# Two graph-attention layers on one core: six weight buffers, bank-by-bank scores over the transposed weights, two c buffers

## The chip, the cores and the metric

The kernel runs on one core of one Trainium2 chip. The metric is the device time of one execution in microseconds (us). The kernel before the change took 4322.22 us, the median of three runs (4315.53 to 4325.43).

The engines are named as the profile names them: PE (TensorE matmuls, with PEld for its weight loads), DVE (VectorE), ACT (ScalarE), POOL (GpSimd) and SP (SyncE, which issues most DMAs). Each has its own queue and works it in order; they wait for each other through semaphores.

## The reference

`x` is 8 images of 2048 rows and 256 columns, `adj` a 2048 x 2048 mask. Each layer attends over rows, adds its input and normalizes. Cut to what is computed:

```
# layer 0, eight heads of 32 columns
x_proj = einsum('bnd,hdf->bhnf', x, W)
e = leaky_relu(e_src[..., :, None] + e_dst[..., None, :], 0.2)
e = e + softplus(beta_tilde) * log(adj + 1e-6)
e = where(adj > 0, e, most_negative)
h = einsum('bhij,bhjf->bhif', softmax(e), x_proj)
x = layernorm(x + concat_heads(h) @ W_out.T)

# layer 1, one head of 256 columns
e = leaky_relu(einsum('bnd,bmd->bnm', x @ W1, x @ W2), 0.2)
e = where(adj > 0, e, -1e12)
x = layernorm(x + relu(softmax(e) @ (x @ W3)))
```

All of it is float32. Layer 1 of an image needs all rows of that image's layer 0.

## The kernel before, in words

**Layer 0 as units.** The exponential of a leaky ReLU of a sum is written as a maximum of two products, so that no exponential of a 2048 x 2048 matrix is needed. The work is cut into units `(hp, jt)`: a pair of heads `hp` (4 per image) and a tile `jt` of 128 neighbours (16). There are 64 units per image and 512 in all. `Gat.step` makes one: for each of the two heads, DVE computes the 128 x 2048 weights `s` (L375) from a row tile `c` (the heads' query factors, spread over the partitions by a DMA, L313), a scalar per partition `re`, and a transposed mask tile `mt` (1 MB, L202, loaded anew for every unit). PE then multiplies `s` into `val` and `den` (L407, `products`): these are matmuls with 32 columns of weights, four of which run side by side in the array. In `SUMMED` tiles the denominator is instead summed on DVE into `d` (L386), the first one on ACT (L392), and only the sum goes through PE. A unit's two `s` tiles come from a ring with tag "s" of four buffers (L374), so DVE can be two units ahead of PE. A pair of heads reads two `c` tiles in all its 16 units; the ring "c" has three buffers (L312). In the last unit of a pair, right behind each head's L375, the next `c` load is put on SP's queue. `finish` and `output` close a pair and an image (division, projection `y` L477, normalization).

**Layer 1 as row tiles.** `Dot` works on the image whose layer 0 is done, one tile of 128 rows at a time, 16 per image. `scores(it)` makes four banks `e` of 512 columns on PE (L538), ACT writes each through a Prelu into the 128 x 2048 tile `p` (L540), DVE masks it and takes the row maximum in one operation (L543), and ACT takes the exponential (L546). `step` then turns `p` back, 128 x 128 at a time (transposes on PE, L561, copied by ACT into `pts`, L563), multiplies the turned weights into `acc` (L577), and ACT and DVE divide, add and normalize (L582 to L585). Scores are made one row tile ahead: `step` for tile `it` holds `scores(it + 1)`, which writes the other of two `p` buffers. The turned weights have two `pts` buffers, so a turn of bank g + 1 stands on PE between the `acc` matmuls of banks g - 1 and g:

```
pt = turned(0)
...
    self.scores(it + 1)
fill(1)
for g in range(NB):
    now, pt = pt, turned(g + 1) if g + 1 < NB else None
    # 4 acc matmuls from now
fill(2)
```

Every fourth step also makes `h1` for the next four row tiles (`queries`, L528).

**How the two layers interleave.** Image 0 runs its layer 0 alone, together with the projections of all other images (L268) and the making of the masks. From then on, layer 1 of image b - 1 and layer 0 of image b share the queues: `fill(k)` in `Dot.step` calls `layer_0`, which runs so many units of the next image at that place. In the 13 middle row tiles of an image, `n` is 3 or 4 and the units stand as `(0, n - 2, 2)`. Between two images the projections `y`, the turns `tr` and `h3` of the finished layer 0 stand between groups of two units. The last image's layer 1 has nothing beside it (the tail).

**What sets the order.** PE's queue is in program order (a manual schedule), and SP's from image 1 on. The order of DVE and ACT is set by the framework's scheduler, within what the data and buffers allow. Three PSUM banks (`ps`, tag "mm") rotate over all matmul results but `acc`, `val` and `den`.

**Other rings.** Tag "p" (two buffers) holds `p`, and at the start the first rows of x and the mask tiles `m`. Tag "pt" (two) holds `pts` and some start-up tiles. Tag "v" (three) holds the projected values of a head pair, loaded in the middle of the pair before.

Of the kernel before, what the change touches and what calls it, by code (L numbers as in the profile page):

```python
# [27 lines left out]
def kernel(  # L28
# [50 lines left out]

    def mm_tile(name):  # L80
        return ps.tile([P, BK], F32, tag="mm", name=name)
# [43 lines left out]
    first_x = [wide.tile([P, NT // 2, D], F32, tag="p", name="xr", bufs=2) for _ in range(2)]  # L125
# [8 lines left out]
    def later_weights():  # L134

        nc.sync.dma_start(w3s, w3.rearrange("(k p) d -> p k d", p=P))
        w1t, w2t = (chunk.tile([P, KC, D], F32, tag="pt", name=name, bufs=2) for name in ("w1t", "w2t"))
# [40 lines left out]
    def make_m(jt):  # L178
# [3 lines left out]
        m = wide.tile([P, NT, P], F32, tag="p", name="m", bufs=2)  # L182
# [51 lines left out]
    class Gat:  # L234
# [12 lines left out]
        def scores_first(self, xt):  # L247
# [7 lines left out]
            s = chunk.tile([P, BK], F32, tag="pt", name="scores", bufs=2)  # L255
# [46 lines left out]
        def load(self, hp):  # L302
            self.v[hp] = chunk.tile([P, NT, HP * DH], F32, tag="v", name="v", bufs=3)
            nc.sync.dma_start(self.v[hp], v_d[self.b, hp])
# [5 lines left out]
        def query_rows(self, h):  # L310

            c = wide_tile("c", "c", 3)  # L312
            nc.sync.dma_start(c, c_d[self.b, h:h + 1, :].to_broadcast([P, N]))  # L313
            return c

        def load_ahead(self):
# [6 lines left out]
            for _ in range(3):  # L323
                self.cs_ahead.append(next(self.c_loads))
                self.mts.append(next(self.mt_loads))
            self.mts.append(next(self.mt_loads))
# [13 lines left out]
        def step(self, count=1):  # L340

            for _ in range(count):
# [29 lines left out]
                for a in range(HP):  # L372
                    h = hp * HP + a
                    sa = wide_tile("s", "s", 4)  # L374
# [140 lines left out]
    class Dot:  # L515


        def __init__(self, gat):
            self.b, self.x1t, self.h3 = gat.b, gat.x1t, gat.h3
            self.at = 0  # L520
            self.queries(0)
# [10 lines left out]
        def scores(self, it):  # L532
            pen = mask(it, self.b == 0)
            p = wide_tile("p", "p", 2)
            for c in range(NB):
                t = mm_tile("e")
# [10 lines left out]
            self.ahead = p, den  # L547

        def step(self, fill=lambda k: None):


            it, (p, den) = self.at, self.ahead
# [4 lines left out]

            def turned(g):
# [3 lines left out]
                pt = chunk.tile([P, BK], F32, tag="pt", name="pts", bufs=2)  # L562
                nc.scalar.copy(pt, t)  # L563
                return pt

            pt = turned(0)
            if it + 1 < NT:
                if (it + 1) % IG == 0:
                    self.queries((it + 1) // IG)
                self.scores(it + 1)  # L570
            fill(1)
            acc = pacc.tile([P, D], F32, tag="acc", name="acc")
            for g in range(NB):
                now, pt = pt, turned(g + 1) if g + 1 < NB else None
                for k in range(IG):
                    j = g * IG + k
                    nc.tensor.matmul(acc, now[:, ts(k, P)], self.h3[:, j, :], start=(j == 0), stop=(j == NT - 1))  # L577
            fill(2)
# [30 lines left out]
    def others():  # L609
# [18 lines left out]
        for n, (gat, g) in enumerate(groups):  # L628
            if g == 0:
                gat.begin()  # L630
            v = chunk.tile([P, NP, IG, HP * DH], F32, tag="v", name="v", bufs=3)
# [32 lines left out]
    for b in range(1, B + 1):  # L664
# [13 lines left out]
        else:  # L678

            dot.step(lambda k: layer_0((0, 2, 2)[k]))  # L680
# [57 lines left out]
```

The softmax here doesn't subtract the row's maximum and nothing guards it: scores larger than these inputs give would overflow.

## Time and profile before

| What | us |
|---|---|
| median of three runs (lowest, highest) | 4322.22 (4315.53, 4325.43) |
| the profiled execution | 4319.21 |
| its span | 4317.4 |
| PE busy | 4191.7 (97%) |
| DVE busy | 3704.8 (86%) |
| ACT busy | 1657.5 (38%) |
| s operations on DVE (L375), 1024 of them | 2355.5 |
| d operations on DVE (L386), 318 | 738.5 |
| mask operations on DVE (L543), 128 | 292.4 |
| 1 MB loads of mt / of c | 496 / 64 |

The table is of one profiled execution. Its time and its span differ by 1.8 us, which lie around the first and the last instruction. Busy time is what an engine spent inside instructions, and matmul ends are modelled, so a busy PE may still have gaps between the starts of its matmuls. Granted clock of TensorE: 0.994 of full speed over the span. The span has three parts: up to about 560 us image 0, from there to about 3880 us seven times the same cycle of about 475 us, then the tail.

### The profile page before, as it was taken

Reading aid. Unit: us, or ns where it says so; the run is one execution under the profiler, and the core shown is the slowest. Engines: PE = TensorE matmul, PEld = TensorE weight load, DVE = VectorE, ACT = ScalarE, POOL = GpSimd, SP = SyncE. Lnnn points to the kernel's source line nnn. Section 1 sums busy time; section 2 is a strip of 40 time slices with the busy share of each in tenths; the row PEclk is TensorE's granted clock in tenths of the full one; section 3 lists DMA queues with packets and bytes.
Section 4 is the critical chain, followed back from the end, with each engine's and each line's share of the span. In section 5 each row is a group of like instructions: output and inputs, shape, how many; then the busy total and the mean of one; then the engine's idle time right before and its main releaser. Section 6 shows DMA issues by size and latency. Waiting matters only on the chain. (4 is left out here: it accounts for less than half of the span.)

```text
span 4317.4 us, 58896 instructions
## 1 busy us (share of the span) xinstructions
PE 4191.7 (97%) x24640; PEld 2202.1 (51%) x24640; DVE 3704.8 (86%) x2468; ACT 1657.5 (38%) x3019; POOL 9.5 (0%) x14
## 2 busy tenths in 40 slices
PE   7999999999999999999999999999999999999999
PEld 5444455454454545544554544555455445545766
DVE  7878888998899989999899998999899998999222
ACT  7522233333333333333343334333333333433554
POOL 0000000000000000000000000000000000000000
PEclk9999999999999999999999999999999999999999
DMA  8979756666555554556555564555545565544211
GB/s 272 308 258 319 273 198 210 225 229 209 184 191 192 201 203 180 179 184 227 187 193 186 189 207 183 192 190 206 202 176 181 186 226 185 198 171 146 81 50 41
DMA packets 267946, 843.50 MB, mean 195 GB/s; under 512 B 32672, under 2 KB 165792, under 8 KB 193952
## 3 DMA queue, kind: packets, MB, share of 16 engines
q1 hardware_dynamic: 232352, 806.17, 53.0%
q10 hardware_dynamic: 35328, 33.56, 2.3%
q8 instruction: 193, 3.16, 0.3%
q14 instruction: 73, 0.60, 0.0%
HBM read 763.76 MB, written 75.37 MB: 194 GB/s over the span
## 5 line engine op out<-in xcount | busy, mean ns | idle before, releaser
L375 DVE SCALAR_TENSOR_TENSOR s<-c,re,mt 128x2048 f32<-128x2048 f32 x1024 | 2355.5, 2343 | 150.3 <-PE den L407 65.6
L407 PE MATMUL val<-s,v 128*32 128x512 f32 x8192 | 1024.5, 602 | 56.7 <-DVE s L375 56.5
L577 PE MATMUL acc<-h,pts 128*128 128x256 f32 x4096 | 955.9, 381 | 18.5 <-ACT pts L563 18.5
L538 PE MATMUL e<-x1t,h 128*128 128x512 f32 x2048 | 904.0, 594 | 4.6 <-ACT pts L563 4.5
L577 PEld LDWEIGHTS acc<-h,pts 128*128 128x128 f32 x4096 | 746.9, 190 | 119.4 <-ACT pts L563 34.2
L386 DVE SCALAR_TENSOR_TENSOR d<-s,re,d 128x2048 f32<-128x2048 f32 x318 | 738.5, 2342 | 0.0
L407 PE MATMUL den<-s,re 128*32 128x512 f32 x5216 | 664.1, 597 | 0.0
L538 PEld LDWEIGHTS e<-x1t,h 128*128 128x128 f32 x2048 | 379.0, 190 | 451.6 <-issue 413.5
L407 PEld LDWEIGHTS val<-s,v 128*32 128x32 f32 x8192 | 245.5, 110 | 675.0 <-issue 519.9
L563 ACT COPY pts<-pt 128x512 f32<-128x512 f32 x512 | 295.4, 582 | 663.5 <-PE pt L561 660.3
L540 ACT ACTIVATE p<-e 128x512 f32<-128x512 f32 x512 | 302.6, 595 | 426.1 <-PE e L538 412.7
L543 DVE CUSTOM_DVE_ANT_0 p<-p,pen 128x2048 f32<-128x2048 f32 x128 | 292.4, 2284 | 198.7 <-ACT p L540 198.6
L407 PEld LDWEIGHTS den<-s,re 128*32 128x32 f32 x5216 | 181.5, 111 | 396.4 <-issue 394.6
L561 PEld LDWEIGHTS pt<-ident,p 128*128 128x128 f32 x2048 | 238.5, 141 | 214.4 <-issue 173.9
L546 ACT ACTIVATE p<-p,neg 128x2048 f32<-128x2048 f32 x128 | 256.7, 2005 | 232.2 <-DVE neg L543 232.2
L561 PE MATMUL pt<-ident,p 128*128 128x128 f32 x2048 | 317.7, 278 | 0.0
L582 ACT ACTIVATE z<-acc,rec 128x256 f32<-128x256 f32 x128 | 60.7, 474 | 391.6 <-PE acc L577 259.4
L583 DVE TENSOR_TENSOR z<-z,x1r 128x256 f32<-128x256 f32 x128 | 53.8, 420 | 142.9 <-ACT z L582 142.8
L392 ACT ACTIVATE d<-s,re 128x2048 f32<-128x2048 f32 x54 | 107.9, 2011 | 80.0 <-PE den L407 66.3
L268 PE MATMUL proj<-wp,xt 128*128 128x272 f32 (+1 forms) x512 | 132.5, 404 | 4.8 <-ACT v L270 3.2
L528 PE MATMUL h1p<-x1t,w 128*128 128x512 f32 x256 | 117.0, 595 | 9.4 <-ACT x1t L503 9.4
L270 ACT COPY v<-proj 128x256 f32<-128x256 f32 x128 | 47.0, 375 | 202.5 <-PE proj L268 197.5
(88 smaller groups left out, 1919.8 us busy)
## 6 DMA issues: line engine op xcount, KB each, us to landing
mt<-mt_d SPq DMA_DIRECT2D x496, 1024.0 KB
c<-c_d SPq DMA_DIRECT2D x64, 1024.0 KB
pen<-pen_d SPq DMA_DIRECT2D x112, 512.0 KB
xg<-in_x_dram SPq DMA_DIRECT2D x60, 512.0 KB
adj_t<-in_adj_dram SPq DMA_DIRECT2D x16, 1024.0 KB
mt_d<-mt SPq DMA_DIRECT2D x16, 1024.0 KB
rb<-rec_d SPq DMA_DIRECT2D x128, 128.0 KB
x_d<-ht ACTq DMA_DIRECT2D x32, 512.0 KB
```

The costliest lines, as they stand in the source:

```text
L268: nc.tensor.matmul(t[:, 0:cols], xt[:, kc, ts(it % IG, P)], wp[:, kc, 0:cols], start=(kc == 0), stop=(kc == KC - 1))
L375: nc.vector.scalar_tensor_tensor(sa, self.cs[a], self.re[:, 0, jt, h:h + 1], mt, ALU.max, ALU.mult)
L386: nc.vector.scalar_tensor_tensor(d, sa, e[:, jt - 1, h:h + 1], d, ALU.mult, ALU.add)
L407: nc.tensor.matmul(dst[ts(q, DH), ts(c, BK)], weights[q % 2], s[q % 2][:, ds(q // 2 * HALF + c * BK, BK)], start=start, stop=stop)
L528: nc.tensor.matmul(t, w12[:, kc, ts(dc, P)], self.x1t[:, kc, ts(g, BK)], start=(kc == 0), stop=(kc == KC - 1))
L538: nc.tensor.matmul(t, self.h1[:, kc, ts(it % IG, P)], self.x1t[:, kc, ts(c, BK)], start=(kc == 0), stop=(kc == KC - 1))
L540: nc.scalar.activation(p[:, ts(c, BK)], t, AF.Prelu, alpha=ALPHA)
L543: nc.vector.tensor_tensor_reduce(p, p, pen, -1.0, FMAX, ALU.add, ALU.min, neg)
L546: nc.scalar.activation(p, p, AF.Exp, bias=neg, scale=-1.0, accum_out=den)
L561: nc.tensor.transpose(t[:, ts(k, P)], p[:, ts(g * IG + k, P)], ident)
L563: nc.scalar.copy(pt, t)
L577: nc.tensor.matmul(acc, now[:, ts(k, P)], self.h3[:, j, :], start=(j == 0), stop=(j == NT - 1))
```

## The change

The ring of `s` gets six buffers (three units). `p` becomes one tile, kept in the pool `whole`. The four banks of turned weights get a `pts` buffer each. `scores` takes a function that it calls ahead of each bank: in `step` this is `turned`, so that PE turns bank c of the old `p` and then makes bank c of the new scores, whose Prelu writes over the old bank. All 16 `acc` matmuls follow in one piece. `fill` has two places instead of three, and the units of a row tile stand together behind `acc`. To make room, `c` goes from three buffers to two, `v` from three to two, and the first rows of x and the tiles `m` move to the ring "s". `load_ahead` loads two `c` and four `mt` tiles ahead, where it loaded three and four.

The diff, without the repeated renames:

```diff
@@ pools
+    p_all = whole.tile([P, N], F32, tag="p", name="p")
...
-    first_x = [wide.tile([P, NT // 2, D], F32, tag="p", name="xr", bufs=2) for _ in range(2)]
+    first_x = [wide.tile([P, NT // 2, D], F32, tag="s", name="xr", bufs=6) for _ in range(2)]
...
-        m = wide.tile([P, NT, P], F32, tag="p", name="m", bufs=2)
+        m = wide.tile([P, NT, P], F32, tag="s", name="m", bufs=6)
@@ Gat
-            self.v[hp] = chunk.tile([P, NT, HP * DH], F32, tag="v", name="v", bufs=3)
+            self.v[hp] = chunk.tile([P, NT, HP * DH], F32, tag="v", name="v", bufs=2)
...
-            c = wide_tile("c", "c", 3)
+            c = wide_tile("c", "c", 2)
...
-            for _ in range(3):
+            for _ in range(HP):
                 self.cs_ahead.append(next(self.c_loads))
                 self.mts.append(next(self.mt_loads))
-            self.mts.append(next(self.mt_loads))
+            for _ in range(2):
+                self.mts.append(next(self.mt_loads))
...
-                    sa = wide_tile("s", "s", 4)
+                    sa = wide_tile("s", "s", 6)
@@ Dot
+            self.p = p_all
             self.queries(0)
...
-        def scores(self, it):
-            pen = mask(it, self.b == 0)
-            p = wide_tile("p", "p", 2)
+        def scores(self, it, between=lambda c: None):
+            pen, p = mask(it, self.b == 0), self.p
             for c in range(NB):
+                between(c)
                 t = mm_tile("e")
...
-            self.ahead = p, den
+            self.ahead = den
@@ Dot.step
             fill(0)
+            pts = []
             def turned(g):
                 t = mm_tile("pt")
                 for k in range(IG):
                     nc.tensor.transpose(t[:, ts(k, P)], p[:, ts(g * IG + k, P)], ident)
-                pt = chunk.tile([P, BK], F32, tag="pt", name="pts", bufs=2)
+                pt = chunk.tile([P, BK], F32, tag="pt", name="pts", bufs=NB)
                 nc.scalar.copy(pt, t)
-                return pt
-            pt = turned(0)
+                pts.append(pt)
             if it + 1 < NT:
                 if (it + 1) % IG == 0:
                     self.queries((it + 1) // IG)
-                self.scores(it + 1)
-            fill(1)
+                self.scores(it + 1, turned)
+            else:
+                for g in range(NB):
+                    turned(g)
             acc = pacc.tile([P, D], F32, tag="acc", name="acc")
             for g in range(NB):
-                now, pt = pt, turned(g + 1) if g + 1 < NB else None
                 for k in range(IG):
                     j = g * IG + k
-                    nc.tensor.matmul(acc, now[:, ts(k, P)], self.h3[:, j, :], start=(j == 0), stop=(j == NT - 1))
-            fill(2)
+                    nc.tensor.matmul(acc, pts[g][:, ts(k, P)], self.h3[:, j, :], start=(j == 0), stop=(j == NT - 1))
+            fill(1)
@@ the interleaving
-            dot.step(lambda k: layer_0((0, 2, 2)[k]))
+            dot.step(lambda k: layer_0((0, 4)[k]))
...
-        dot.step(lambda k: layer_0((2, 0, 2)[k]))
+        dot.step(lambda k: layer_0((2, 2)[k]))
...
-            dot.step(lambda k: layer_0((0, n - 2, 2)[k]))
+            dot.step(lambda k: layer_0((0, n)[k]))
```

More of the change, by code (lines that the diff above doesn't have):

```diff
@@ L136, in later_weights @@
         nc.sync.dma_start(w3s, w3.rearrange("(k p) d -> p k d", p=P))
-        w1t, w2t = (chunk.tile([P, KC, D], F32, tag="pt", name=name, bufs=2) for name in ("w1t", "w2t"))
+        w1t, w2t = (chunk.tile([P, KC, D], F32, tag="pt", name=name, bufs=NB) for name in ("w1t", "w2t"))
         for w, dst in ((w_out, wot), (w1, w1t), (w2, w2t)):
@@ L254, in scores_first @@
                                      start=(kc == 0), stop=(kc == KC - 1))
-            s = chunk.tile([P, BK], F32, tag="pt", name="scores", bufs=2)
+            s = chunk.tile([P, BK], F32, tag="pt", name="scores", bufs=NB)
             nc.scalar.copy(s, t)
@@ L546, in scores @@
             nc.scalar.activation(p, p, AF.Exp, bias=neg, scale=-1.0, accum_out=den)
-            self.ahead = p, den
+            self.ahead = den
         def step(self, fill=lambda k: None):
-            it, (p, den) = self.at, self.ahead
+            it, p, den = self.at, self.p, self.ahead
             self.at += 1
@@ L630, in others @@
                 gat.begin()
-            v = chunk.tile([P, NP, IG, HP * DH], F32, tag="v", name="v", bufs=3)
+            v = chunk.tile([P, NP, IG, HP * DH], F32, tag="v", name="v", bufs=2)
             for k in range(IG):
```

## The prediction

> **What bounds the kernel now.** I read the busy shares first, then the windows of one image cycle, then the waits inside the stretch in which both layers run, last the groups. Busy time of PE and DVE over the whole span:
>
> ```profile
> PE 4191.7 (97%) x24640; PEld 2202.1 (51%) x24640; DVE 3704.8 (86%) x2468; ACT 1657.5 (38%) x3019; POOL 9.5 (0%) x14
> ```
>
> PE looks like the only limit, but DVE's 86% is an average over a first image and a tail in which it has little to do. From 560 to 3880 us seven images pass, each in about 475 us (3320 / 7). One of them, cut at its mask operations (L543): first the thirteen row tiles that carry 44 layer-0 units, then the change of images (columns: us, then busy us of PE, PEld, DVE, ACT, POOL):
>
> ```profile
> 2145.30:2488.70 343.40, 339.80 (x1951) 173.57 (x1953) 332.58 (x213) 129.41 (x227) 0.00 (x0) 1.00 0.52 187
> 2488.70:2620.00 131.30, 122.72 (x789) 63.47 (x782) 111.27 (x77) 45.13 (x77) 0.00 (x0) 0.99 0.60 209
> ```
>
> In the long part DVE works 332.6 of 343.4 us and PE 339.8: **two engines at their limits**, coupled by four s buffers, that is two units of lead. In the short part both have holes. Who waits for whom from 560 to 3880 us:
>
> ```profile
> DVE z L583 <- ACT z L582: 73.7, 37, 3.4
> DVE p L543 <- ACT p L540: 67.7, 16, 9.4
> DVE s L375 <- DMA mt<-mt_d: 43.0, 22, 4.9
> ...
> DVE s L375 <- DMA c<-c_d: 4.3, 5, 3.1
> ...
> PE val L407 <- DVE s L375: 40.5, 33, 3.3
> PE acc L577 <- ACT pts L563: 17.9, 34, 1.3
> PE h1p L528 <- ACT x1t L503: 9.4, 7, 1.5
> PE e L538 <- ACT pts L563: 4.5, 6, 1.0
> ```
>
> PE's waits come to about 74 us, the first for s, the second for the copy of transposed weights. The c loads are almost free today (4.3 us). The groups that set the prices:
>
> ```profile
> L375 DVE SCALAR_TENSOR_TENSOR s<-c,re,mt 128x2048 f32<-128x2048 f32 x1024 | 2355.5, 2343 | 150.3 <-PE den L407 65.6
> L577 PE MATMUL acc<-h,pts 128*128 128x256 f32 x4096 | 955.9, 381 | 18.5 <-ACT pts L563 18.5
> L386 DVE SCALAR_TENSOR_TENSOR d<-s,re,d 128x2048 f32<-128x2048 f32 x318 | 738.5, 2342 | 0.0
> L561 PE MATMUL pt<-ident,p 128*128 128x128 f32 x2048 | 317.7, 278 | 0.0
> ```
>
> Instructions overlap, so I price by the spacing of starts in the trace: an s or d operation 2.26 us; PE records 0.429 (e), 0.216 (acc), 0.109 (pt), and 0.43 for four val or den records, which run side by side.
>
> [...] from the last 32-wide den record to the first transpose 0.523 us pass where 0.409 are usual (0.114 lost), from the last e record to the first val 0.522 for 0.429 (0.093): 0.21 us per visit to the units. [...] here 53 c loads land 4.3 to 9.1 us after issue, median 6.3, and I use 6.3. [...]
>
> **The change part by part.** No arithmetic goes or comes; the counts of matmuls, DVE and ACT operations and bytes stay.
>
> *One visit to the units instead of two.* A row tile ran: turn bank 0, scores, n-2 units, turn banks 1 to 3 between the acc groups, 2 units. It becomes: scores and turns bank by bank, acc, n units. In 13 row tiles of each of 7 images, and one more at each change of images, a visit falls away: (13 + 1) x 7 x 0.21 = 20.6 us, if PE is the limit there.
>
> *Turns before acc.* acc no longer follows a copy that has just been issued: the last e bank (4 x 0.43 = 1.7 us) covers the last copy (0.58 us). PE's acc waits, 17.9 us, go. The new rotation through three PSUM banks gives a bank back one e group later (1.7 us plus a turn of 0.44), against ACT's 0.6 us per copy; ACT is busy 38% and its queue keeps copies and Prelus in PE's order, so I take 0; if an ACT block of 2 us (L392, L546) falls in, up to 0.5 us in each of 112 row tiles, 56 us at worst.
>
> *p in one buffer.* Prelu of bank c waits for the transposes of bank c, which PE's queue has ahead of it: 0. The chain to the next turns is Prelu 0.7, mask 2.3, Exp 2.2 and gaps, 5.5 us in the tail's timeline; after the change acc alone (32 x 0.216 = 6.9 us) must cover it where no units run. It does, with 1.4 us over: the tail (3890 to 4290 us, PE busy 397.7 of 400) stays.
>
> *Six s buffers.* The new instruction order has all three units of a row tile ahead of the next mask operation on DVE; PE reaches them 7 us after the scores. Walking six row tiles with the prices above, DVE reaches the mask 1 to 4 us late and PE waits 0.5 us in 155. Long part: PE's own work is 13 x (6.9 e + 6.9 acc + 1.75 pt) + 10.3 h1p + 69 val or den groups x 1.72 = 331, with visits and bank turns 335 after and 338 before; 343.4 less 2.7 (13 visits) less 2.9 (acc and e waits) is 337.8. DVE needs 332.6 + 1.8 for c + 3 forced waits for z = 337.4. Two equal limits never mesh fully; I take 339.5, **4 us less per image**, between 0 (DVE wins) and 6. Short part: PE waits 6.6 us for s there, and one more unit of lead holds 2 x 2.26 = 4.5 us of DVE work; less 0.5 for c, **4 per image**, between -1 and 8.
>
> *Two c buffers.* Both rows of a pair are now loaded after the last reader of the old ones. From the new order I take what stands on DVE between that reader and the first user: 2.3, 4.6, 7.1 and 5.0 us at the four boundaries of an image. Against 6.3 + 0.05 this is a wait of 4.1, 1.8, 0 and 1.4, 7.3 us per image. Behind the waiting operation stand all later s operations, the mask and z; PE waits for them through s. The 4.1 falls where PE has some 16 us of turns, h1p and e ahead of the next unit: hidden. The 1.8 and 1.4 are in the sums above. In image 0 three boundaries wait about 6 us each (loads land in 7 to 9 there); PE spends some 5.6 us per unit and has up to three in hand: I take 4 us in all, 0 to 18.
>
> *The rest.* v in two buffers: its load waits for a unit that PE has finished by then (an s three units on cannot be made earlier): 0; were it late, PE would lose the 4.5 us of its landing 28 times, 126 us. SP's queue keeps its order; the c loads stand behind mt loads that wait for earlier s. mt waits (43 us) may grow by 10 with longer DVE bursts, inside the ranges given. m and the first x in the s ring fall on the same turn of two plus four buffers: 0, +-5.
>
> Sum: -4 x 7 - 4 x 7 + 4 = **-52 us**. The visits and the acc waits are contained in the -4 of the long part, not added. The profiled execution took 4319.2 (span 4317.4), 3 us under the median of 4322.2: **4267 us**.
>
> **Rivals.** (1) *The c wait takes the place of the s wait; slower.* If DVE is the only limit, every wait for c reaches the end: 7 x 7.3 + 3 x 6 = 69 us, visits and acc waits are worth nothing, and only part of the lead's 28 is kept: 4360 (4335 to 4388). It decides once DVE reaches the mask more than about 9 us after the scores: then PE finds no s. For it: DVE's 332.6 of 343.4. Against: DVE idles over 200 us from 560 to 3880, much of it forced by z, p and mt. (2) *Full decoupling.* All PE waits but h1p's go (63 us), with 20 for the visits: 4236. Against it: DVE's share in the long part. (3) *The lead is not used*, because DVE's order pins z and the mask; only half the visits and acc waits are won and c eats the rest: 4310 to 4328, no change. The order speaks against this, since it places the extra unit ahead of the mask.
>
> **How the numbers follow.** The main case (4245 to 4305) 0.56, rival 2 0.14, rival 3 0.08, rival 1 0.22. Faster and slower mean over 0.2% (8.6 us, about what a measurement of this kernel can tell): faster 0.70, same 0.08, slower 0.22. The range runs from 4222 (rival 2 with the short part's 8) to 4345, inside rival 1; within the likeliest sign alone it is 4222 to 4305.
>
> **What would show it.** PE waits of acc for pts near 0; PE waits for s down from 40 to some 15 us; DVE waits for c up from 4 to about 45; the long part 338 to 341 us, the short 126 to 129; the tail unchanged. Wrong if PE's s waits rise in the long part (rival 1), if e or pt waits for ACT copies exceed 10 us, or if val waits for v.

## Result and profile after

The changed kernel takes 4320.45 us (median, 4312.68 to 4329.83) against 4322.4 for the kernel before on the same chip: ratio 0.9996, 95% interval 0.9988 to 1.0005, **no change**. The forecast was 4267. The profiled execution has a span of 4312.8 us (before 4317.4).

The page's busy times of the changed kernel, and its costliest groups (busy us, mean ns of one | idle just before them, and what ended most of it):

```profile
PE 4174.6 (97%) x24640; PEld 2225.8 (52%) x24640; DVE 3712.1 (86%) x2468; ACT 1634.4 (38%) x3019; POOL 9.5 (0%) x14
...
L378 DVE SCALAR_TENSOR_TENSOR s<-c,re,mt 128x2048 f32<-128x2048 f32 x1024 | 2361.2, 2342 | 193.8 <-PE den L410 68.6
L410 PE MATMUL val<-s,v 128*32 128x512 f32 x8192 | 1030.7, 604 | 78.9 <-DVE s L378 77.7
...
L585 PE MATMUL acc<-h,pts 128*128 128x256 f32 x4096 | 905.0, 379 | 0.0
```

The idle time ahead of acc is gone (18.5 us before), but 78.9 us now stand ahead of val (56.7 before), nearly all of it for s. The windows of the same image cycle, cut at its mask operations:

```profile
2147.87:2492.54 344.67, 339.65 (x1965) 178.08 (x1965) 327.92 (x209) 126.88 (x227) 0.00 (x0) 1.00 0.53 187
2492.54:2615.61 123.07, 116.33 (x746) 59.70 (x748) 109.48 (x76) 40.76 (x71) 0.00 (x0) 0.97 0.61 214
```

The prediction's second window, to 2620.00, ends 6.9 us behind the mask operation at 2613.07. Cut there, the change of images in the kernel before is this one, so that 123.1 us stand against 124.4 and not against 131.3:

```profile
2488.71:2613.07 124.36, 115.78 (x740) 60.87 (x736) 104.33 (x73) 42.45 (x74) 0.00 (x0) 0.99 0.62 216
```

The long part is 344.7 us, where 343.4 stood and 338 to 341 was forecast: PE is busy as long as before and DVE stands 16.8 us in it instead of 10.8. Who waits for whom from 560 to 3880 us:

```profile
DVE s L378 <- PE den L410: 42.2, 23, 3.7
DVE s L378 <- DMA mt<-mt_d: 34.2, 35, 2.5
DVE s L378 <- DMA c<-c_d: 32.6, 26, 2.9
DVE z L591 <- ACT z L590: 31.3, 43, 2.1
DVE rec L588 <- ACT p L551: 24.3, 14, 2.2
...
PE val L410 <- DVE s L378: 55.9, 52, 4.4
PE e L543 <- ACT pts L571: 7.5, 8, 1.1
```

PE's waits of acc are gone, as forecast; its waits for s rose from 40.5 to 55.9, where 15 was forecast. Two of the prediction's signs of being wrong are there: in the long part shown, PE waits 2.3 us for s instead of 0.7, and its waits ahead of e for ScalarE's copies come to 13.2 us (7.5 for pts, 5.7 for h), over the 10 that were set. DVE waits less for z and p, but more for a free s slot (the den rows: 22 before), for c (4.3 before) and for the exponential ahead of the reciprocal (4.1 before).

The profiled executions differ by 4.6 us, and the start of each image's layer 1 ("first e", the first score matmul) shows where. Image 0 ends 9.2 us later (first e at 585.4 instead of 576.2). The changed kernel gets this back, and a little more, at about 2 us an image. The tail is unchanged (270.9 us from the last image's first e to the end, 271.2 before).

### The profile page after: what moved, and what is told of

It reads as the page before. It is cut to its first block, busy times and chain, and to the rows that moved or that the text cites. A ratio compares the mean times of both kernels' runs of the same rounds, so it can differ in the third digit from the quotient of the medians.

```text
span 4312.8 us, 58556 instructions
## 1 busy us (share of the span) xinstructions
PE 4174.6 (97%) x24640; PEld 2225.8 (52%) x24640; DVE 3712.1 (86%) x2468; ACT 1634.4 (38%) x3019; POOL 9.5 (0%) x14
## 4 chain that ended last, share of the span: by engine, by line
PE 62%; DVE 20%; issue 8%; DMA 6%; ACT 3%; SPq 0%; ACTq 0%; DVEq 0%; POOLq 0%; POOL 0%
PE acc L585 15%; PE e L543 14%; PE val L410 13%; DVE s L378 13%; PE den L410 9%; PE pt L569 4%; DVE d L389 3%; DMA mt<-mt_d 3%; PE proj L270 2%; DMA c<-c_d 2%; PE h1p L532 2%; PE y L480 2%; DVE p L548 1%; PE h3p L511 1%; DVE ht L482 1%
## 5 line engine op out<-in xcount | busy, mean ns | idle before, releaser
L410 PE MATMUL val<-s,v 128*32 128x512 f32 x8192 | 1030.7, 604 | 78.9 <-DVE s L378 77.7
L543 PE MATMUL e<-x1t,h 128*128 128x512 f32 x2048 | 963.6, 594 | 15.2 <-ACT h L534 7.7
L585 PE MATMUL acc<-h,pts 128*128 128x256 f32 x4096 | 905.0, 379 | 0.0
L585 PEld LDWEIGHTS acc<-h,pts 128*128 128x128 f32 x4096 | 777.6, 190 | 156.6 <-issue 57.4
L410 PE MATMUL den<-s,re 128*32 128x512 f32 x5216 | 675.0, 598 | 0.0
L410 PEld LDWEIGHTS val<-s,v 128*32 128x32 f32 x8192 | 257.0, 110 | 695.2 <-issue 515.6
L543 PEld LDWEIGHTS e<-x1t,h 128*128 128x128 f32 x2048 | 350.8, 190 | 278.6 <-issue 248.4
L226 ACT ACTIVATE f<-mv,eps_ln 128x1 f32<-128x1 f32 x128 | 37.8, 295 | 336.8 <-DVE mv L224 336.8
L511 PE MATMUL h3p<-w3s,x1t 128*128 128x256 f32 x512 | 122.4, 382 | 1.7 <-ACT x1t L506 1.7
```

Of the source, the lines that this page charges most:

```text
L410: nc.tensor.matmul(dst[ts(q, DH), ts(c, BK)], weights[q % 2], s[q % 2][:, ds(q // 2 * HALF + c * BK, BK)], start=start, stop=stop)
L511: nc.tensor.matmul(t[:, ts(i, D)], x1t[:, kc, ts(2 * (j - lag) + i, P)], w3s[:, kc, :], start=(kc == 0), stop=(kc == KC - 1))
L543: nc.tensor.matmul(t, self.h1[:, kc, ts(it % IG, P)], self.x1t[:, kc, ts(c, BK)], start=(kc == 0), stop=(kc == KC - 1))
L585: nc.tensor.matmul(acc, pts[g][:, ts(k, P)], self.h3[:, j, :], start=(j == 0), stop=(j == NT - 1))
```

## Experiments

Times are medians, ratios are to the kernel before on the same chip with 95% intervals. "Six cycles" is the stretch from the first e of image 1 to that of image 7; its figure comes from one profiled execution, and two kernels that differ in image 0 alone gave 2939.5 and 2947.3, so 8 us there mean nothing. Five of its cycles are whole; the last is shorter, as no layer-0 unit is left at its end.

Four theories stood at the start. T1: DVE's own work and the waits pinned in its order limit the image cycle, and PE's savings come back as waits for s. T2: the waits for c took the gain. T3: single operations stand at a bad place in DVE's order (the reciprocal behind the exponential, the first y ahead of unit 6). T4: m in the ring of s delays image 0. T5, that the single visit uses up the six s buffers, came with the second group of runs.

### Is it image 0, c, the reciprocal, or DVE's amount of work?

**m in a tile of its own**, `m_pair`, which has two slots in the place of h3 and takes the first x as well.

```diff
-        m = wide.tile([P, NT, P], F32, tag="s", name="m", bufs=6)
+        m = m_pair[:, jt % 2]
```

> The changed kernel with one part undone: m and the first x of image 0 get a tile of their own with two slots, as before the change, in place of slots in the ring of s. The first e record of image 1 came 9.2 us later after the change (585.4 against 576.2). T4 (the shared ring pushes the m operations ahead of the first s on DVE and so delays image 0): first e back at about 576, the whole 7 to 10 us shorter than the changed kernel, about 4311, and the cycles of the later images as in the changed kernel. Rival (the start-up's 9 us come from the c loads of image 0, of which only two are in flight): first e stays at 583 to 586 and the time stays within 3 us of the changed kernel.

4310.5 us, ratio 0.9977 (0.9969 to 0.9985). The first e is back at 576.2 us. T4 holds in this: m in the ring of s costs some 9 us in image 0. (In this run's profiled execution, at 4315.4 us one of its slower ones, the cycles lose them again, within the 8 us that mean nothing.) How the ring does it is not shown. T4 said that m operations move ahead of the first s, but the traces have fewer of them there, four against five in the kernel before, and the first s starts at 37.1 us against 36.4. Two of DVE's waits in the first 580 us of the changed kernel follow; with m apart the first is 3.7 us and the second is not there, while m waits 12.1 us for PE instead:

```profile
DVE m L185 <- DMA adj_t<-in_adj_dram: 11.4, 3, 5.2
...
DVE s L378 <- PE proj L270: 10.3, 2, 7.6
```

**No reloading of c**, in the changed kernel and, as a control, in the kernel before.

```diff
-            self.c_loads = (gats[b].query_rows(h) for b in range(self.b, B) for h in range(H))
+            self.c_loads = (gats[b].query_rows(h) for b in range(self.b, self.b + 1) for h in range(HP))
...
-                        self.cs = [self.cs_ahead.pop(0) for _ in range(HP)]
-                    else:
+                        kept[:] = [self.cs_ahead.pop(0) for _ in range(HP)] if self.cs_ahead else kept
+                        self.cs = list(kept)
+                    elif hp == 0:
```

In both kernels 4 of the 64 loads are left, those of the first pair in image 0 and in image 1, so more goes than the three quarters of the first expectation. The control also loads two rows ahead instead of three.

> The changed kernel without the reloading of c: c is loaded for the pairs of the images 0 and for the first pair of image 1 only, later pairs multiply the c that is in the buffers (this leaves out about three quarters of the loads, and the attention of layer 0 uses stale rows). T2 (the waits for c in two buffers took the gain): DVE's 32.6 us of c waits between 560 and 3880 us go, PE's waits for s fall from 56 to about 30, and the time falls by 25 to 35 us. T1 (DVE's own work and its other pinned waits are the limit, c is one wait of several): DVE's c waits go too, but the mt, z and den waits that stand beside them grow, the gain is 8 to 20 us. If c is hidden behind PE altogether: within 4 us of the changed kernel.

> Control for the run of the changed kernel without c loads (4288.3 us, 32 below the changed kernel): the kernel before with the same part left out, c loaded only for the first pair of image 0 and of image 1, so that attention of layer 0 uses stale rows later; three c buffers as before. T2 (the two c buffers took the gain): the kernel before hardly waits for c (4.3 us between 560 and 3880, 6.6 in image 0), so it gains at most 5 to 8 us, about 4312 to 4318, and without c the change is worth 24 to 30 us. Rival (c loads cost as much with three buffers, by traffic or by what waits in SP's queue behind them): it gains 15 to 30 us too, 4290 to 4305, and the buffers for c are not where the gain went.

Changed kernel: 4288.3 us, ratio 0.9929 (0.9917 to 0.9942). Kernel before: 4307.22, ratio 0.9972 (0.9962 to 0.9983). So 32 us go in one and 12 in the other. The kernel before gains all of it in image 0 (first e 11.9 us earlier, and 12.0 at the end), so that part comes from the loads themselves and not from the number of buffers. The changed kernel gains 14.6 there and 24.0 at the end. If the loads cost both kernels the same apart from the buffers, the two buffers cost about 20 us by the medians, and about 12 by the profiles. The 32 us lie in the range of T2, but PE's waits for s fall only to 46.4 where T2 had about 30. T2 explains part of the missing gain, not most: without any c load the change would still be worth only 19 us. DVE's and PE's waits of the changed kernel without c loads, 560 to 3880 us, show where the freed time went:

```profile
DVE s L379 <- DMA mt<-mt_d: 57.0, 34, 3.9
...
DVE p L549 <- ACT p L546: 37.5, 17, 12.6
...
PE val L411 <- DVE s L379: 46.4, 49, 2.0
```

The c rows (32.6) are gone, mt grew by 23 and p by 17: DVE's free time moved on to the next wait.

**The reciprocal on ScalarE.**

```diff
-            nc.vector.reciprocal(rec, den)
+            nc.scalar.activation(rec, den, AF.Ln)
+            nc.scalar.activation(rec, rec, AF.Exp, scale=-1.0)
```

> The changed kernel with the reciprocal of layer 1's denominators taken from DVE: ScalarE forms it as exp of minus the logarithm, two operations of 128x1 behind the exponential of the mask, in each of 128 row tiles (same value up to rounding). In the changed kernel DVE waits 24.3 us for the exponential at the reciprocal (14 waits of 2.2 us) between 560 and 3880. T3 (DVE's order pins the reciprocal behind the exponential and holds up the s behind it, PE then waits for s): these waits go, PE's waits for s fall from 56 to 35 to 45, 12 to 20 us shorter. T1 (DVE's free time only moves to the next wait): the reciprocal's waits go, DVE's waits for mt, den or c rise by about as much, under 6 us gained. Loss of up to 10 us if the two operations hold up ScalarE's copies and PE's pt or e then wait.

4311.95 us, ratio 0.9982 (0.9974 to 0.9991): 6 to 9 us less than the changed kernel, between the two cases. The 24.3 us of waits at the reciprocal are gone, DVE's waits for z rose from 31 to 48.5 and PE's waits for s fell only from 55.9 to 52.3. Mostly T1.

**Less of the denominator on DVE.**

```diff
-    SUMMED += [[(2, 4, 10, 13)] + [tuple(range(0, NT, 2))] * (NP - 1)] * (B - 2)
+    SUMMED += [[(2, 4, 10, 13)] + [tuple(range(0, NT - 2, 2))] * (NP - 1)] * (B - 2)
```

> The changed kernel with less of layer 0's denominator on DVE: of the eight j tiles of the pairs 1 to 3 of the images 2 to 7 that DVE adds up, the last (14) goes back to PE, so in 18 pairs two d operations of 2.26 us (81 us of DVE work in all) fall away and PE gets some four den records more, 1.7 us in each (31 us in all). T1 (DVE is what limits the image cycle of the changed kernel, PE's share of the change's gain comes back as waits for s): the time falls by 15 to 50 us although PE has more to do. Rival (PE is the limit and its waits for s are incidental): the time rises by 20 to 31 us. Between: within 5 us, both engines limit.

4313.31 us, ratio 0.9979 (0.9972 to 0.9986): about 7 us less, just outside the middle case. DVE's work fell by 79 us, but its waits for c rose from 32.6 to 87.7: the d operations of tile 14 were what stood between the old and the new c rows. So this run took away a cover as well as work, and does not tell T1 from its rival.

**All of the denominator on PE**, in both kernels.

```diff
-    SUMMED = [[()] * NP, [()] + [(0, 3, 6, 8, 11, 14)] * (NP - 1)]
-    SUMMED += [[(2, 4, 10, 13)] + [tuple(range(0, NT, 2))] * (NP - 1)] * (B - 2)
+    SUMMED = [[()] * NP] * B
```

> The kernel before with none of layer 0's denominators added up on DVE (all 318 d operations go, PE does every denominator itself), for comparison with the changed kernel under the same edit. DVE loses 738 us of work and PE gains some 0.86 us for every pair of records moved, so that PE alone is the limit of the image cycle. Expected about 4500 to 4650 us; PE's waits for s nearly 0 in either theory. The number that counts is the difference to the same edit of the changed kernel.

> The changed kernel with none of layer 0's denominators added up on DVE, as in the run of the kernel before with this edit. PE is then the limit of the image cycle. T1 (PE's share of the gain is real, and it comes back as waits for s because DVE is full): freed from DVE the change now shows it: 20 us of visits and 18 us of acc waits, 30 to 45 us below the kernel before with the same edit, less up to 9 in image 0. Rival (the visits and acc waits were never worth their price on PE): within 12 us of each other.

4498.63 us with the kernel before (ratio 1.042, 1.0406 to 1.0434), 4478.86 with the changed one (1.0371, 1.0357 to 1.0385): 20 us between them, less than the 30 to 45 expected. In the profiles image 0 loses 16.6 us in the changed kernel (first e 589.1 against 572.5), and behind it the change wins 28.6, of which 12.0 are left at the end; the profiled execution of the changed one is its slowest. With DVE busy only 70% of the stretch from 560 to 3880 us, PE's waits for s are 6.3 and 5.1 us. So PE's share of the gain is real where DVE has time. That in the kernel as it stands it comes back as waits for s fits this, and the next runs test it.

### Is it the order of the units?

**The new order with the buffers of before, and with five s.**

```diff
-            c = wide_tile("c", "c", 2)
+            c = wide_tile("c", "c", 3)
...
-                    sa = wide_tile("s", "s", 6)
+                    sa = wide_tile("s", "s", 4)
```

The other run has five s, and v stays at two. In both, three c rows are loaded ahead and m has its own tile.

> The changed kernel with one of the six s buffers given back to c (five s, three c, three c rows loaded ahead as before the change) and m in a tile of its own. The order of units and turns stays. T2 (c in two buffers took the gain): against the changed kernel with m alone moved (4310.5) DVE's c waits of 31.6 us between 560 and 3880 fall under 8 and the time falls by 10 to 25 us, to 4286 to 4300. T1 (DVE's other pinned waits take over): c waits fall, mt, z and p waits rise, the time stays within 5 us of 4310. If six s buffers carried a gain that five lose: PE's waits for s rise from 56 to over 70 and the time rises above 4316.

> The new order of work alone, with the buffers of the kernel before: one visit to the units per row tile, turns between the scores, p in one buffer, m in a tile of its own, but four s, three c and three v buffers and three c rows loaded ahead. Five s and three c buffers gave 4417.7 with PE waiting 105 us for s between 560 and 3880. T5 (the two extra s buffers are the price of the single visit, since its units stand back to back on PE and take s in one burst; they are no gain of their own): PE's waits for s are above those of five buffers, 130 to 250 us, and the time 4430 to 4560. Rival (five is bad only because five slots and two heads per unit do not divide; four is no worse than in the kernel before): PE's waits for s 40 to 70, the time 4300 to 4330.

Five s: 4417.68 us, ratio 1.0229 (1.0215 to 1.0243). Four s and three v: 4584.09, ratio 1.0603 (1.0589 to 1.0618). Both are far outside what was expected of c: with three c and five s buffers the c waits fell to 3.4 us as they should, and the time rose by 107 us over the changed kernel with m apart. PE's waits for s from 560 to 3880 us, with four s buffers:

```profile
PE val L410 <- DVE s L378: 186.9, 206, 5.4
```

They are 186.9 us with four buffers, 105.2 with five and 55.9 with six (55.8 with m apart). T5 holds: the single visit eats buffers.

**Two visits per row tile again, with six s buffers.** Everything else of the change stays.

```diff
+            fill(1)
             acc = pacc.tile([P, D], F32, tag="acc", name="acc")
...
-            fill(1)
+            fill(2)
...
-            dot.step(lambda k: layer_0((0, 4)[k]))
+            dot.step(lambda k: layer_0((0, 2, 2)[k]))
...
-            dot.step(lambda k: layer_0((0, n)[k]))
+            dot.step(lambda k: layer_0((0, n - 2, 2)[k]))
```

> The changed kernel with its six s buffers and its turns between the scores, but the units of a row tile in two visits again, the first ahead of acc and the last two behind it. T5 (six s buffers only pay for the burst of the single visit): with the burst gone, PE's waits for s fall from 56 to 20 to 40 between 560 and 3880, which about pays for the 20 us of a second visit: 4305 to 4325, within 8 us of the changed kernel. If the lead of six buffers is worth something beyond the burst: the waits for s fall under 15 and the time falls to 4290 to 4305. If the waits for s are pinned by DVE's own order and do not depend on the visits: they stay above 50 and the time is 4335 to 4345.

**4253.07 us, ratio 0.9846 (0.9832 to 0.9859)**: 68 us under the kernel before, better than any of the three cases. Its windows of the same image cycle, and the waits from 560 to 3880 us:

```profile
2119.53:2460.99 341.46, 340.07 (x1972) 174.72 (x1968) 328.85 (x210) 128.92 (x229) 0.00 (x0) 1.00 0.54 190
2460.99:2573.43 112.44, 110.76 (x728) 59.50 (x724) 105.94 (x72) 38.84 (x70) 0.00 (x0) 1.00 0.65 229
```

```profile
DVE p L548 <- ACT p L545: 46.7, 27, 10.5
DVE s L378 <- DMA c<-c_d: 40.7, 28, 2.9
DVE s L378 <- PE den L410: 23.2, 19, 3.7
...
DVE z L592 <- ACT z L591: 5.1, 11, 0.7
...
DVE rec L589 <- ACT p L551: 2.2, 1, 2.2
...
PE e L543 <- ACT pts L571: 13.6, 8, 2.1
PE val L410 <- DVE s L378: 10.8, 10, 2.0
```

PE's waits for s fall from 55.9 to 10.8; DVE's waits for a free slot, z and the reciprocal fall from 98 to 31. Its waits for the scores ahead of the mask (20.4 in the changed kernel) and for c are longer, and PE hardly waits for s all the same. The change of images takes 112.4 us instead of 123.1, although the visits of the long part are what differs most.

**Two visits with the buffers of before**: the edit above together with four s, three c, three v and m apart.

> Two visits with the new turns between the scores and p in one buffer, but with the buffers of the kernel before (four s, three c, three v, m in a tile of its own). One visit with these buffers gave 4584.1. This is the turns' own share of the 68 us that two visits with six s buffers gain over the kernel before. T6 (six s buffers carry most of it, the turns are worth the acc waits at most): 4300 to 4320, PE's waits for s 35 to 50 between 560 and 3880. Rival (the turns between the scores carry it): 4255 to 4290. The two visits with four buffers below 4330 would in any case show that the 262 us of one visit with four buffers come from the visit.

4329.47 us, ratio 1.0023 (1.0014 to 1.0031), slower than the kernel before and 9 us above the range of T6. T6 holds in its point: with four s buffers, the turns between the scores and p in one buffer carry nothing. Six s buffers with the old turns were not run, so what the turns do there is open. PE and DVE of this kernel, 560 to 3880 us:

```profile
DVE p L548 <- ACT p L545: 96.9, 29, 9.3
...
PE val L410 <- DVE s L378: 41.8, 37, 3.0
PE e L543 <- ACT pts L571: 16.4, 7, 2.4
```

The 17.9 us of acc waits became 16.4 us of e waits for the same copies (4.5 before), and DVE waits 29 us more for the scores ahead of its mask.

**Two visits only ahead of the change of images.**

```diff
-            dot.step(lambda k: layer_0((0, 4)[k]))
+            dot.step(lambda k: layer_0((0, 2, 2)[k]))
...
-            dot.step(lambda k: layer_0((0, n)[k]))
+            dot.step(lambda k: layer_0((0, 0, n)[k]))
```

> The changed kernel with two visits in one row tile per image only, the last one ahead of the change of images (two units ahead of acc and two behind, instead of four behind); the thirteen other row tiles keep the single visit. Two visits everywhere gave 4253.1 and took 47 us out of the change of images and 14 us out of the long part. T5a (it is the burst of four units there that leaves DVE late at the change of images): most of it comes back, 4265 to 4290, and PE's waits for s at the units 6, 15 and 63 fall from 67 us together to under 30. T5b (the single visits of the long part leave DVE behind by the time the change begins, since DVE stands with full s buffers in each row tile): within 10 us of the changed kernel, 4310 to 4325.

4320.54 us, ratio 0.9998 (0.9991 to 1.0005): nothing. T5a falls. T5b is left: the change of images is short in the kernel with two visits because of how far ahead DVE is when it arrives there; the table of the lead further on agrees.

**The single visit ahead of acc** instead of behind it.

```diff
+            fill(1)
             acc = pacc.tile([P, D], F32, tag="acc", name="acc")
...
-            fill(1)
```

> The changed kernel with the single visit moved: all units of a row tile stand ahead of acc instead of behind it. The burst stays, the place changes, and the saved mode switches stay saved. T5 (the burst itself, three or four units at once, drains the six s buffers and leaves DVE standing with full ones for the rest of the row tile): 4300 to 4340, PE's waits for s 45 us or more. Rival T7 (the place is what costs: behind acc the units come too late after the scores and the reciprocal and z stand on DVE behind them): 4225 to 4260, as with two visits or better by the switches.

4433.81 us, ratio 1.0263 (1.0249 to 1.0277), worse than either case. The place is not the remedy. PE takes the units right behind the scores. The mask, which needs these scores, stands on DVE ahead of the s operations of the next units, so DVE waits for the scores and then PE for s:

```profile
DVE p L548 <- ACT p L545: 208.2, 55, 11.8
...
PE val L410 <- DVE s L378: 109.4, 110, 4.1
```

**Units 6 and 7 ahead of y** at the change of images, where PE waited longest for s in the changed kernel.

```diff
-        layer_0(2)
+        layer_0(4 if dot is not None else 2)
...
-            if g < NB + 1:
+            if g < NB + (b == 1):
```

> The changed kernel with the units 6 and 7 of an image moved ahead of the first y product at the change of images (four units stand there, none behind the last group). In the changed kernel DVE's order has the first add of ht, which waits for y, ahead of the s of unit 6, and unit 6 is where PE waits longest for s: 36.6 us in six images. T3 (that pinned order is what keeps the lead from being used there): waits at unit 6 fall under 12 and the time falls by 8 to 25 us. Rival (DVE has no time to spare there whatever the order): the waits move to the units 7 to 10 or to y, within 5 us of the changed kernel. Loss of up to 10 us if PE's y then comes later and the h3p products wait for ht.

4359.5 us, ratio 1.009 (1.0076 to 1.0103): 39 us slower than the changed kernel, more than any case gave. PE's idle time ahead of unit 6 (the gap ends with the unit's first val record) fell only from 23.4 to 19.5 us in six images (the expectation's 36.6 is another count, by the spacing of starts), unit 11 got 21.8 us of it, and PE's h1p waits 15.1 us for ScalarE's h. As T3's remedy this fails. It does not settle T3, since the edit also makes a burst of four units and leaves none behind the last group.

### What the runs point to

**Tile 14 in place of 13** in the sums of pair 0.

```diff
-    SUMMED += [[(2, 4, 10, 13)] + [tuple(range(0, NT, 2))] * (NP - 1)] * (B - 2)
+    SUMMED += [[(2, 4, 10, 14)] + [tuple(range(0, NT, 2))] * (NP - 1)] * (B - 2)
```

> The changed kernel with one tuple altered: pair 0 of the images 2 to 7 adds up its tiles 2, 4, 10 and 14 on DVE instead of 2, 4, 10 and 13. The work stays; the two d operations of tile 14 (4.5 us) now stand between the last s that reads the old c rows and the first that reads the new ones, where DVE waited 4.8 us in one image. The steady part of the c waits was worth 9 us by the run without c loads. T2 in what is left of it: DVE's c waits fall from 32.6 to 12 to 20 us between 560 and 3880 and the time falls by 3 to 9 us. T1 (the wait only moves to mt or den): c waits fall and the time stays within 3 us. A loss of up to 8 us if the closing product for pair 0 now waits for the later sum.

4304.89 us, ratio 0.9966 (0.9953 to 0.9978), some 13 to 16 us under the changed kernel and more than expected; the c waits fell from 32.6 to 21.0. The same 4.5 us of DVE work, put where a load is under way, are worth about 2 us an image. That is more than the c waits alone lost; PE's waits for s fell from 55.9 to 44.2.

**Two visits, m apart and tile 14 together.**

> The version that the runs point to: the changed kernel with two visits (4253.1 alone), m in a tile of its own (8 to 10 us in image 0) and pair 0 adding up tile 14 instead of 13 (15 us under the changed kernel, alone). If the three add up: 4226 to 4236. If the last is hidden once DVE has its lead: 4238 to 4247. PE is the limit then, its waits for s under 12 us between 560 and 3880.

**4239.7 us, ratio 0.9815 (0.9802 to 0.9828)**, 81 us under both kernels. The three do not add up: the first e is at 578.0 us (587.2 with two visits alone), so m keeps its 9 us, and of the 13 us between the two kernels some 4 are left for tile 14. That its c waits were already hidden fits this and is not tested apart. PE's waits for s are 4.6 us from 560 to 3880.

## Why the prediction was wrong

The four kernels that combine visits and buffers hold the answer (medians in us; all have the new turns, and those with four s buffers have m apart and three v):

| | four s, three c | six s, two c |
|---|---|---|
| two visits | 4329.5 | 4253.1 |
| one visit | 4584.1 | 4320.5 (the change) |

The turns and p in one buffer cost 8.5 us (4321 to 4329.5). The buffers then gain 76, although they carry a loss of about 9 for m and some for c. The single visit takes 67 of it back.

**"One visit to the units instead of two" is the step that failed.** It was priced on PE alone, at 20.6 us of mode switches gained "if PE is the limit there". A mode switch is a change between 32-wide and 128-wide records: in the traces of both kernels the first pt behind a den record starts after 0.523 us instead of 0.409, and the first val behind acc after 0.309 instead of 0.216 (medians). The switches are saved: 166 fewer in six cycles, at some 0.105 us each 17 us. But with one visit PE takes all units of a row tile in one burst and none for the rest of it. A timeline of DVE in the changed kernel, in one row tile, shows what follows (start us, busy us, operation by the profile's name, and in brackets the idle time before it):

```profile
2251.64 2.29 DVE L548 CUSTOM_DVE_ANT_0 p<-p,pen 128x2048 f32<-128x2048 f32 x1
2253.85 0.08 DVE L548 DVE_READ_ACCUMULATOR2_ANT neg<- 128x1 f32 x1
2256.10 0.16 DVE L588 RECIPROCAL rec<-den 128x1 f32<-128x1 f32 x1 [2.16 <-ACT p L551]
...
2260.14 2.35 DVE L378 SCALAR_TENSOR_TENSOR s<-c,re,mt 128x2048 f32<-128x2048 f32 x1 [1.62 <-PE den L410]
```

Behind the mask the next operation in DVE's order is the reciprocal, and it waits for the exponential. Then the next s waits for a slot, since PE has only just begun the burst that empties them. PE does not wait in this row tile; DVE's lead pays for it. The same row tile with two visits:

```profile
2224.54 2.28 DVE L548 CUSTOM_DVE_ANT_0 p<-p,pen 128x2048 f32<-128x2048 f32 x1
2226.75 0.08 DVE L548 DVE_READ_ACCUMULATOR2_ANT neg<- 128x1 f32 x1
2226.75 4.61 DVE L378 SCALAR_TENSOR_TENSOR s<-c,re,mt 128x2048 f32<-128x2048 f32 x2
2231.28 2.35 DVE L389 SCALAR_TENSOR_TENSOR d<-s,re,d 128x2048 f32<-128x2048 f32 x1
```

The first visit has freed slots ahead of acc, the s operations stand behind the mask, and nothing waits in these lines. The two kernels differ in the visits alone, so the visit sets both where slots come free and what stands behind the mask.

The lead shows it. Finished s pairs that PE has not yet begun, at the first e record of a row tile, as a mean of six images (counted in the trace; one s alone counts as a half):

| row tile | 6 | 9 | 10 | 11 | 12 | 13 | 14 | 15 |
|---|---|---|---|---|---|---|---|---|
| before | 0.5 | 0.0 | 0.5 | 0.5 | 1.0 | 0.0 | 0.5 | 0.0 |
| changed kernel | 1.0 | 0.5 | 0.0 | 1.0 | 1.0 | 0.5 | 0.0 | 0.4 |
| two visits, six s | 1.6 | 1.0 | 1.0 | 1.0 | 2.0 | 1.0 | 1.0 | 0.8 |

The changed kernel has a lead in the first row tiles and has spent it by the tenth. It has one again at 11 and 12 and none at 14, so it enters the change of images with next to nothing in hand. Two visits keep about one unit throughout. Over six cycles (DVE's waits and PE's waits of val for s as the profile has them, gaps counted in the trace):

| | six cycles | DVE's waits | PE's waits for s | gaps ahead of val and den |
|---|---|---|---|---|
| before | 2951.1 | 213 | 32.8 | 58 |
| changed kernel | 2939.5 | 191 | 46.5 | 77 |
| two visits, six s | 2878.8 | 144 | 4.9 | 17 |
| two visits, four s | 2962.3 | 221 | 34.2 | 59 |
| one visit, four s | 3189.3 | 425 | 174.8 | 249 |

The last column is the spacing of PE's starts beyond the usual one; it holds the waits and the slow stretches behind them. From the changed kernel to two visits it falls by about 60 us, and the cycles by 60.7. That the two agree is partly chance, since other terms nearly cancel. Some 17 us of switches are paid again. Against that, 56 fewer groups of four val or den records come apart into one and three (66 in the changed kernel, 10 with two visits), an estimated 23 us at 0.41 us each, the median step in the traces from a group's last record to the next group. That the burst does this by the full slots and the pinned reciprocal and z together is read from the waits. The share of each is not separated: the reciprocal alone was worth 6 to 9 us.

The other steps:

- **Six s buffers.** The walk of six row tiles had DVE reach the mask "1 to 4 us late" and PE wait 0.5 us in 155. It took the visit and the buffers as two gains. The buffers gain more than the 28 us set down for the short part, but only with two visits. With one visit, six buffers are just enough to stand where the kernel before stood with four. A walk of six row tiles also could not show a lead that is spent later in the image.
- **Turns before acc.** The acc waits went, as said, but the copies are waited for one record later: e waits for pts are 16.4 us with two visits and four s. The step had named this risk and taken it at 0. With four s buffers its net worth, p in one buffer included, is a loss of 8.5 us.
- **Two c buffers.** The mechanism was right, and the forecast of 45 us of DVE waits met 32.6. What they cost was mis-sized: an estimated 12 to 20 us where the sum had 4 in image 0 and little elsewhere. That DVE had no lead to hide them behind fits the run with two visits, where DVE waits 40.7 us for c and PE only 10.8 for s; it is not tested apart. The sum used the landing of the c loads as measured in the kernel before, 6.3 us at the median.
- **m in the s ring**, taken as 0 with 5 to either side: 8 to 10 us. The working looked only at which slot comes free. What the ring delays is open: DVE's order at the start differs, and two of its waits are longer, as shown above.
- **p in one buffer, v in two.** Nothing of weight: pt waits 2.2 us for ScalarE's exponential, and no val wait for v appears.
- **The cycle.** 475 us was a miscount: the stretch from 560 to 3880 us holds 6.6 cycles of about 503 us (501 after the change), and the two windows together left out 29 us that are dense with PE work. The short part was 124.4 us when cut at the mask operations; it fell by 1.3 us where 4 was forecast. Neither slip enters the sum, which counts gains per image.
- **The tail** stayed, as said.

Rival 3 has the time, "4310 to 4328, no change", and half of the mechanism: DVE's order does pin z and the reciprocal. What it lacked is that the visit makes this so. Rival 1 named DVE as the limit. Its c wait is real, but at 12 to 20 us it is a smaller part of the missing 52, and the time did not rise.

## What to carry to other kernels

When one engine feeds another through a few buffers, the places where the consumer takes from them belong to the price: fewer, longer visits save switches (here some 0.105 us each) but can need more buffers. Here one visit of three or four units used up the two buffers that were added with it. Price a merged visit on the producer's queue too: list what stands there between the last free slot and the next visit, and walk the lead to the end of the cycle, not for its first few steps. A change in two parts that move one quantity in opposite ways should be forecast as a table of both parts, and run as one.

## What the runs showed of the hardware

A gap on PE can cost more than its own length. At the change of images in the changed kernel PE waits for s at unit 6, and the granted clock of TensorE is 0.61 and 0.71 in the two windows from 2530 us on (columns: us, then busy us of PE, PEld, DVE, ACT, POOL, granted clock, DMA share, GB/s):

```profile
2525.00:2530.00 5.00, 3.69 (x16) 2.32 (x14) 3.82 (x4) 0.00 (x0) 0.00 (x0) 1.00 0.03 10
2530.00:2535.00 5.00, 2.59 (x13) 0.59 (x16) 5.00 (x4) 0.51 (x2) 0.00 (x0) 0.61 0.21 59
2535.00:2540.00 5.00, 5.00 (x37) 1.27 (x33) 4.04 (x4) 2.08 (x4) 0.00 (x0) 0.71 0.54 184
```

PE stands for 3.7 us in these windows, in two gaps:

```profile
2529.19 1.04 PE L410 MATMUL val<-s,v 128*32 128x512 f32 x2 [1.31 <-DVE s L378]
2532.65 2.78 PE L410 MATMUL val<-s,v 128*32 128x512 f32 x11 [2.41 <-DVE s L378]
```

The same stretch, cut where the clock changes, with half as long a piece ahead of it:

```profile
2527.69:2531.10 3.41, 1.23 (x3) 0.14 (x2) 3.41 (x4) 0.00 (x0) 0.00 (x0) 1.00 0.00 0
2531.10:2537.93 6.83, 5.28 (x28) 1.35 (x32) 6.69 (x5) 2.59 (x6) 0.00 (x0) 0.50 0.42 155
```

For 6.83 us the clock is 0.50, and groups of four val or den records start every 0.85 us where 0.43 is usual. From 2532.65 to 2537.77 six such groups pass in 5.12 us, so an estimated 2.5 us are lost (5.12 less 6 x 0.43) on top of the 3.7 of waiting; the rest of the slow stretch falls into the second gap. Over five changes of images the mean granted clock is 0.97 to 0.99 in the changed kernel and before, and 1.00 in all five with two visits, where PE has no such gap. What makes the clock drop is not shown: in the 3.41 us ahead of the drop PE was still busy for 1.23, and its longest gap is 2.4 us. Nor does every wait have a slow stretch behind it. In the same change of images PE waits for s in two gaps of 1.2 us between 2590.1 and 2593.5 us, and in the row tiles of an earlier image it waits 2.2 us for ScalarE's h, up to 1398.61; in both places the clock stays at 1.00. Where a slow stretch follows, it belongs to the price of the wait: here an estimated 2.5 us on top of 3.7.
